# AdaLN-conditioned FFN with LoRA experts on one core: lora_B split a product sooner, the first transposes later, T4's casts in the third group

## The chip, the cores and the metric

The kernel runs on one core of one Trainium2 chip. The metric is the device time of one execution in microseconds; lower is better. All numbers below are of the kernel before the change.

## The reference

```python
h = einsum('bct,bcd->bdt', x, weights[condition])      # (64, 64, 1024), a 64x64 matrix per sample
logits = h @ gate_w.T + expert_bias                     # 4 experts, top 1 by argmax
base   = einsum('bth,oh->bto', h, W_up)                 # 1024 x 1024
z      = einsum('nh,erh->ner', h, lora_A)               # rank 8 for each of 4 experts
delta  = einsum('ner,ehr->neh', z, lora_B) * 1.0, of the chosen expert alone
out    = x + base + delta
```

All of it is in float32. Two samples together make one tile of 128 rows, so there are 32 row tiles ("rows" below) of 128 x 1024.

## The kernel before

The order of the two linear maps is turned round. First x is multiplied with one wide matrix w, which holds the gate (4 columns), lora_A (32) and W_up (1024), 1060 columns in all. The result u is then multiplied, row tile by row tile, with a block-diagonal matrix `bd` of the two samples' 64 x 64 matrices. That gives the logits, the low-rank z and the base output together.

Float32 precision comes from splitting every operand into a high part (float32r, a cast on ACT) and a low part (a subtraction on DVE), and from three matmuls per product: high x high, low x high, high x low. In the profile the tiles named `hB`, `lB`, `hT`, `lT` are the two parts of blocks of w, `ah` and `al` those of x, `uh` and `ul` those of u, `b` those of lora_B.

The rows go in 16 groups g of two (a and b). In a group, x is a 2 x 2 grid of blocks (A11, A12 for row a, A21, A22 for row b; halves of the 1024 input columns) and w a 2 x 2 grid (B11 to B22, halves of 530 output columns). Groups 0 and 1 (`eight`) take eight block products. Groups 2 to 15 (`seven`) take seven, a Strassen-like scheme with sums S1 to S4 of x's blocks and T1 = B12 - B11, T3 = B22 - B12, T2 = B22 - T1, T4 = B21 - T2 of w's blocks. The T blocks are made once, during groups 0 and 1: `begin_b` loads a block from an SP queue, `next_b` negates it in place on ACT (profile: ACT ACTIVATE T<-T) and then adds another block with an accumulating DMA that POOL issues, and `split_b` makes the high and low parts. Each block has four tiles (k = 0 to 3) of 128 x 530. T2 reuses T1's raw tiles, and T4 reuses T2's. T4 shares its split tiles with B12.

One block product is a "step" s of `product`, with four slices k, each of six matmuls (0.74 us at full clock). The order of all other work is written out by hand: `at(s, k, fn, ...)` makes `fn` be issued right after slice k of step s (k = -1: before the step), and `each` does so for several tiles. Every engine executes its own instructions in that program order. So where a call stands decides what it queues behind on ACT, DVE, POOL and PE.

```python
def product(c, g, a, b, first, hooks):
    for k in range(KH):
        ...                       # six matmuls
        for kk, fn, *args in hooks:
            if kk == k:
                fn(*args)
```

What follows a finished u of a row: `apply` (three matmuls with `bd`, into `o`), `gate` (seven small DVE instructions that choose the expert and leave the masked z), `turn` (PE transposes z; ACT copies it to `zt`, DVE makes the low part), `delta` (one matmul with `b3`, lora_B stacked three times, added to the same `o`), `evict` (ACT copies `o` to `y`; after the third column part POOL adds x by an accumulating DMA and SP writes the output). `finish` is apply, delta and evict. `split_b3` makes b3 on ACT (96 x 1024) and its low part on DVE (32 x 1024) from the raw tile `b3f`, which SP loads in three DMAs.

The steps of group 0 that the change touches are 4 (A11 x B12), 5 (A21 x B12), 6 (A12 x B22) and 7 (A22 x B22). In group 2, T4 is read by the seventh product. `load_half` loads half a row tile of x (`xh`, six buffers); `split_a` makes its two parts.

Of the kernel before, what the change touches and what calls it, by code (L numbers as in the profile page):

```python
# [44 lines left out]
def kernel(  # L45
# [131 lines left out]
    def body(c):  # L177
        return c[:, LEFT : LEFT + NB]
# [7 lines left out]
    def u_split(i, n, src):  # L186
        h, lo = u_tiles(i)
        scalar.copy(h[:, n], src)
        vector.tensor_sub(lo[:, n], src, h[:, n].bitcast(F32))

    def half(hf):
        return slice(NB * hf, NB * hf + NB)

    def u_of(i, hf, c):
        u_split(i, half(hf), body(c))
# [5 lines left out]
    def u_sum(i, hf, c, t):  # L201
        u_add(i, c, t)
        u_split(i, half(hf), ts["u", i])
# [168 lines left out]
    def run(g, order, hooks, c):  # L372
        for s, (n, l, r, first) in enumerate(order):
            if first:
                c[n] = chain()
            for kk, fn, *args in hooks[s]:
                if kk < 0:
                    fn(*args)
            product(c[n], g, l, r, first, hooks[s])
# [4 lines left out]
    def eight(g):  # L384
        a, b = 2 * g, 2 * g + 1
        h = [[] for _ in range(8)]

        def at(s, k, fn, *args):
            h[s].append((k, fn, *args))

        def each(s, k, fn, q, ks, *args):
            for i in ks:
                at(s, k, fn, q, i, *args)

        one, two = (0, 1), (2, 3)
        if g == 0:
            at(0, 0, split_a, g, "A21")
            each(0, 1, split_b, "B21", one)
            at(0, 2, split_a, g, "A12")
            each(0, 3, split_b, "B21", two)  # L400
            each(1, -1, load_b, "B12", range(KH))
            at(1, 0, split_a, g, "A22")
            each(1, 1, split_b, "B12", one)
            each(1, 3, split_b, "B12", two)
            each(1, 3, load_b, "B22", range(KH))
            at(2, 1, split_cond, a)
            at(2, 2, load_b3)
            for i in (2, 3):
                at(2, 3, load_half, i, 0)
            at(3, -1, lambda: u_of(a, 0, c["1"]))  # L410
            at(3, 1, split_cond, b)
            each(3, 2, split_b, "B22", one)
            each(3, 2, begin_b, "T1", range(KH), "B11")
            at(3, 3, apply, a, 0)
            at(3, 3, gate, a)
            at(4, -1, lambda: u_of(b, 0, c["2"]))
            each(4, 1, split_b, "B22", two)
            at(4, 3, turn, a)
            each(4, 3, next_b, "T1", one, "B12")
            for i in (2, 3):  # L420
                at(4, 3, load_half, i, 1)
            at(5, 0, split_b3)
            at(5, 1, delta, a, 0)
            at(5, 1, evict, a, 0)
            at(5, 2, apply, b, 0)
            at(5, 2, gate, b)
            each(5, 2, next_b, "T1", two, "B12")
            at(5, 2, split_a, g + 1, "A11")
            each(5, 3, begin_b, "T3", range(KH), "B12")
            at(6, 2, turn, b)  # L430
            at(6, 2, split_a, g + 1, "A21")
            at(7, -1, lambda: u_of(a, 1, c["3"]))
            at(7, 0, delta, b, 0)
            at(7, 0, evict, b, 0)
            at(7, 1, split_a, g + 1, "A12")
            at(7, 2, finish, a, 1)
            each(7, 2, split_b, "T1", one)
            at(7, 3, finish, a, 2)
            order = (
                ("1", "A11", "B11", True),  # L440
                ("2", "A21", "B11", True),
                ("1", "A12", "B21", False),
                ("2", "A22", "B21", False),
                ("3", "A11", "B12", True),
                ("1", "A21", "B12", True),
                ("3", "A12", "B22", False),
                ("1", "A22", "B22", False),
            )
        else:
            p = a - 1  # L450
            at(0, -1, lambda: u_of(p, 1, cs[g - 1]["1"]))
            at(0, 0, split_a, g, "A22")
            at(0, 3, finish, p, 1)
            at(1, 0, finish, p, 2)
            each(0, 3, next_b, "T3", (0, 1, 2, 3), "B22")
            each(1, 1, split_b, "T1", two)
            at(1, 1, load_cond, a + 2)
            at(1, 1, load_cond, b + 2)
            for i in (b + 2, a + 2):
                at(1, 1, load_half, i, 0)  # L460
            each(1, 3, next_b, "T2", one, "B22", "T1")
            each(2, 1, next_b, "T2", two, "B22", "T1")
            for i in (b + 2, a + 2):
                at(2, 1, load_half, i, 1)
            at(3, -1, lambda: u_of(a, 1, c["1"]))
            each(3, 1, split_b, "T3", one)
            each(3, 3, split_b, "T3", two)
            at(4, -1, lambda: u_of(b, 1, c["2"]))
            at(4, 0, sums, g + 1, "S1")
            at(4, 1, split_cond, a)  # L470
            each(4, 1, split_b, "T2", one)
            each(4, 2, next_b, "T4", one, "B21", "T2")
            at(4, 3, split_cond, b)
            at(5, 0, sums, g + 1, "S2")
            each(5, 1, split_b, "T2", two)
            each(5, 2, next_b, "T4", two, "B21", "T2")
            at(5, 2, split_a, g + 1, "A11")
            at(5, 3, sums, g + 1, "S3")
            at(6, 1, split_a, g + 1, "S2")
            at(6, 2, sums, g + 1, "S4")  # L480
            at(7, -1, lambda: u_of(a, 0, c["3"]))
            each(7, 1, split_b, "T4", one)
            at(7, 3, apply, a, 0)
            at(7, 3, gate, a)
            order = (
                ("1", "A11", "B12", True),
                ("2", "A21", "B12", True),
                ("1", "A12", "B22", False),
                ("2", "A22", "B22", False),
                ("3", "A11", "B11", True),  # L490
                ("1", "A21", "B11", True),
                ("3", "A12", "B21", False),
                ("1", "A22", "B21", False),
            )
        run(g, order, h, c)
        cs[g] = dict(c)


    def seven(g):
        a, b = 2 * g, 2 * g + 1  # L500
# [5 lines left out]
        def at(s, k, fn, *args):  # L506
            h[s].append((k, fn, *args))

        def each(s, k, fn, q, ks, *args):
            for i in ks:  # L510
                at(s, k, fn, q, i, *args)
# [15 lines left out]
        if g == 2:  # L527
            at(0, -1, lambda: u_of(pb, 0, cp["1"]))
            at(0, 2, turn, pa)
            at(1, 0, delta, pa, 0)  # L530
            at(1, 0, evict, pa, 0)
            at(1, 1, finish, pa, 1)
            at(1, 2, finish, pa, 2)
            each(1, 3, split_b, "T4", (2, 3))
            at(1, 3, apply, pb, 0)
            at(1, 3, gate, pb)
            at(2, 3, turn, pb)
        else:
            at(0, -1, lambda: u_sum(pb, 0, cp["2"], ts["t1"]))
            at(0, 1, finish, pa, 1)  # L540
            at(0, 3, finish, pa, 2)
            at(1, 2, apply, pb, 0)
            at(1, 2, gate, pb)
            at(2, 2, turn, pb)
# [102 lines left out]
    for g in range(2):  # L647
        eight(g)
    for g in range(2, NG):
        seven(g)  # L650
# [44 lines left out]
```

## Time and profile before

| what | us |
|---|---|
| median of 6 runs | 433.7 |
| lowest and highest run | 432.87 and 435.58 |
| profiled execution, its own time | 433.73 |
| its span, first to last instruction | 431.7 |
| PE busy (96% of the span) | 416.0 |
| DVE busy (65%) | 279.6 |
| ACT busy (44%) | 190.5 |
| POOL busy (19%) | 80.2 |

The times of single instructions come from the profiled execution, in us from the start of its span. The mean granted clock of PE over the span is 0.988. In the listings, PE is the matmul engine, PEld its weight loads, ACT the scalar engine, DVE the vector engine, POOL and SP the two that issue DMAs here. A row of a timeline gives start, length, engine, line, operation, output<-inputs and shape, and in square brackets the idle time of that engine just before it with what ended it. Nearly all instructions carry line 41, which is the helper that keeps program order, so tiles' names tell them apart.

### The profile page before, as it was taken

What the parts mean: (1) busy time and instruction counts of PE and PEld (TensorE: products, weight loads), DVE (VectorE), ACT (ScalarE), POOL (GpSimd) and SP (SyncE); (2) the same over time, 40 slices, a digit from 0 to 9 for tenths busy, and PEclk for the clock granted to TensorE, in tenths of its full rate; (3) what the DMA queues carried; (4) which work ended last, traced back from release to release, by engine and by line L of the source; (5) the groups of instructions that cost most, each with busy time, mean ns of one, the idle gap of its engine ahead of it and who ended that gap; (6) DMA issues with size and microseconds to landing.
All of it is one profiled execution on the core that took longest, in us unless ns stands there. A gap on an engine that the chain in (4) does not pass through costs nothing.

```text
span 431.7 us, 8164 instructions
## 1 busy us (share of the span) xinstructions
PE 416.0 (96%) x3187; PEld 412.5 (96%) x3187; DVE 279.6 (65%) x631; ACT 190.5 (44%) x425; POOL 80.2 (19%) x97
## 2 busy tenths in 40 slices
PE   8969994999999999999999999999999999999996
PEld 7869993999999999999999999999999999999995
DVE  4845247576676766766676666667666666767656
ACT  4854745535353334435233444533444353433531
POOL 2430722202102020200202020110202011020000
PEclk9989997999999999999999999999999999999999
DMA  7997998345364643535564453446445344665243
GB/s 212 348 347 174 212 208 153 69 114 143 104 172 128 172 127 84 131 96 162 129 171 128 100 130 94 149 129 170 129 118 133 87 144 118 173 155 145 50 99 146
DMA packets 26598, 63.18 MB, mean 146 GB/s; under 512 B 3552, under 2 KB 4832, under 8 KB 26560
## 3 DMA queue, kind: packets, MB, share of 16 engines
q0 software_dynamic: 7680, 21.13, 28.0%
q1 hardware_dynamic: 18880, 41.53, 26.7%
q8 instruction: 25, 0.41, 0.4%
q14 instruction: 13, 0.11, 0.1%
HBM read 45.87 MB, written 16.78 MB: 145 GB/s over the span
## 4 chain that ended last, share of the span: by engine, by line
PE 82%; issue 7%; DMA 5%; POOL 3%; DVE 1%; SPq 1%; ACT 0%; POOLq 0%; DVEq 0%
PE c L41 68%; PE o L41 14%; DMA T<-in_w_dram 4%; POOL wsel L41 1%; POOL T L41 1%; DMA cond_sb<-in_cond_dram 1%; SPq L327 0%; SPq L139 0%; DVE S L41 0%; DVE y L41 0%; DVE usum L41 0%; DVE lT L41 0%; DVE ul L41 0%; ACT hT L41 0%; ACT ah L41 0%
## 5 line engine op out<-in xcount | busy, mean ns | idle before, releaser
L41 PE MATMUL c<-hT,ah 128*128 128x264 f32 x480 | 140.5, 293 | 0.0
L41 PE MATMUL c<-lT,ah 128*128 128x264 f32 x480 | 137.9, 287 | 0.0
L41 PE MATMUL c<-hT,al 128*128 128x264 f32 x480 | 137.8, 287 | 0.0
L41 PE MATMUL c<-hB,ah 128*128 128x264 f32 (+1 forms) x432 | 125.6, 291 | 0.8 <-issue 0.5
L41 PE MATMUL c<-hB,al 128*128 128x264 f32 (+1 forms) x432 | 124.8, 289 | 0.3 <-issue 0.3
L41 PE MATMUL c<-lB,ah 128*128 128x264 f32 (+1 forms) x432 | 124.4, 288 | 0.3 <-DVE lB L41 0.3
L41 PEld LDWEIGHTS c<-lT,ah 128*128 128x128 f32 x480 | 91.6, 191 | 0.0
L41 PEld LDWEIGHTS c<-hT,ah 128*128 128x128 f32 x480 | 91.5, 191 | 0.0
L41 PEld LDWEIGHTS c<-hT,al 128*128 128x128 f32 x480 | 91.4, 191 | 0.0
L41 PEld LDWEIGHTS c<-hB,ah 128*128 128x128 f32 x432 | 82.7, 192 | 1.6 <-ACT ah L41 0.8
L41 PEld LDWEIGHTS c<-lB,ah 128*128 128x128 f32 x432 | 82.8, 192 | 1.0 <-DVE lB L41 1.0
L41 POOL DMA_DIRECT2D y<-in_x_dram x30 | 28.9, 962 | 293.4 <-ACT y L41 293.4
L41 PEld LDWEIGHTS c<-hB,al 128*128 128x128 f32 x432 | 82.3, 190 | 0.6 <-issue 0.5
L41 ACT COPY y<-o 128x354 f32<-128x354 f32 (+2 forms) x90 | 39.9, 443 | 62.1 <-PE o L41 60.3
L41 ACT CAST uh<-usum 128x530 fp32r<-128x530 f32 (+4 forms) x44 | 27.1, 616 | 68.8 <-DVE usum L41 68.7
L41 DVE TENSOR_TENSOR al<-xh,ah 128x512 fp32r<-128x512 f32 (+1 forms) x53 | 34.9, 659 | 31.6 <-ACT ah L41 31.6
L41 DVE TENSOR_TENSOR al<-S,ah 128x512 fp32r<-128x512 f32 x56 | 38.5, 687 | 23.5 <-ACT ah L41 23.5
L41 PE MATMUL o<-uh,bd 128*128 128x354 f32 (+2 forms) x188 | 46.6, 329 | 4.9 <-ACT uh L41 4.8
L41 ACT CAST zt<-o 96x128 fp32r<-96x128 f32 x32 | 8.4, 262 | 85.5 <-PE o L41 85.5
L41 DVE TENSOR_TENSOR ul<-usum,uh 128x530 fp32r<-128x530 f32 (+4 forms) x44 | 30.0, 683 | 19.3 <-ACT uh L41 19.3
L41 POOL DMA_INDIRECT wsel<-in_cw_dram,idx x32 | 35.3, 1102 | 9.9 <-issue 5.2
L41 PEld LDWEIGHTS o<-uh,bd 128*128 128x128 f32 x188 | 30.0, 192 | 5.3 <-issue 5.3
(59 smaller groups left out, 466.7 us busy)
## 6 DMA issues: line engine op xcount, KB each, us to landing
xh<-in_xt_dram SPq DMA_DIRECT2D x63, 256.0 KB
y<-in_x_dram POOLq DMA_DIRECT2D x30, 512.0 KB, 5.6
out_dram<-y SPq DMA_DIRECT2D x30, 512.0 KB
wraw<-in_w_dram SPq DMA_DIRECT2D x16, 265.0 KB
T<-in_w_dram POOLq DMA_DIRECT2D x16, 265.0 KB, 7.4
T<-in_w_dram SPq DMA_DIRECT2D x8, 265.0 KB
y<-in_x_dram SPq DMA_DIRECT2D x2, 512.0 KB
wsel<-in_cw_dram,idx POOLq DMA_INDIRECT x32, 4.9
```

Source lines behind the costliest of these rows:

```text
L41: return lambda *a, **k: self.tc.keep_in_program_order(fn(*a, **k))
```

## The change

In group 0 the split of lora_B (`split_b3`) is issued in step 4 after slice 1, ahead of the last two tiles of B22; it was in step 5 after slice 0, behind T1's first two negations. Those last two B22 splits go from slice 1 to slice 2 of step 4. Row a's transpose, T1's first two negations with their POOL DMAs, and two loads of x go from step 4's last slice to step 5's first. Row a's delta and evict go one slice later (step 5, slice 2). Row b's apply and gate go from step 5, slice 2, to step 6, slice 0; T1's second pair and a split of A11 go one slice later. Row b's transpose goes to slice 3 of step 6, its delta and evict to slice 1 of step 7.

In group 1 the split of T4's first two tiles after slice 1 of step 7 is taken out. In group 2 the first two tiles are split in step 1 after slice 3, where the second two were, and the second two in step 2 after slice 3, registered ahead of row pb's transpose.

The work done, the number of DMAs and the order of the DMA issues on SP and POOL are the same. On PE five blocks change place: row a's transpose and delta stand one slice (six matmuls) later, row b's apply two slices, and row b's transpose and delta one slice.

```diff
@@ eight, g == 0
-            each(4, 1, split_b, "B22", two)
-            at(4, 3, turn, a)
-            each(4, 3, next_b, "T1", one, "B12")
+            at(4, 1, split_b3)
+            each(4, 2, split_b, "B22", two)
+            at(5, 0, turn, a)
+            each(5, 0, next_b, "T1", one, "B12")
             for i in (2, 3):
-                at(4, 3, load_half, i, 1)
-            at(5, 0, split_b3)
-            at(5, 1, delta, a, 0)
-            at(5, 1, evict, a, 0)
-            at(5, 2, apply, b, 0)
-            at(5, 2, gate, b)
-            each(5, 2, next_b, "T1", two, "B12")
-            at(5, 2, split_a, g + 1, "A11")
+                at(5, 0, load_half, i, 1)
+            at(5, 2, delta, a, 0)
+            at(5, 2, evict, a, 0)
+            at(6, 0, apply, b, 0)
+            at(6, 0, gate, b)
+            each(5, 3, next_b, "T1", two, "B12")
+            at(5, 3, split_a, g + 1, "A11")
             each(5, 3, begin_b, "T3", range(KH), "B12")
-            at(6, 2, turn, b)
             at(6, 2, split_a, g + 1, "A21")
+            at(6, 3, turn, b)
             at(7, -1, lambda: u_of(a, 1, c["3"]))
-            at(7, 0, delta, b, 0)
-            at(7, 0, evict, b, 0)
+            at(7, 1, delta, b, 0)
+            at(7, 1, evict, b, 0)
@@ eight, g == 1
-            each(7, 1, split_b, "T4", one)
@@ seven, g == 2
-            each(1, 3, split_b, "T4", (2, 3))
+            each(1, 3, split_b, "T4", (0, 1))
+            each(2, 3, split_b, "T4", (2, 3))
```

## The prediction

> **What bounds the kernel now.** The page comes first: TensorE (PE) is busy 416.0 of 431.7 us, so only its gaps and the clock it is granted can give time back. The list of waits, cut to PE, shows where the gaps are (columns: who waited and for whom, us in total, times, longest).
>
> ```profile
> PE o L41 <- ACT uh L41: 4.8, 1, 4.8
> PE o L41 <- DVE b L41: 3.4, 1, 3.4
> PE o L41 <- DVE ul L41: 1.1, 1, 1.1
> ```
>
> After 72 us there is no PE wait up to 415 us. The change touches the second row (call it wait A) and moves what leads to the first and third (wait B). The timelines of PE, ACT and DVE show how A comes about (start, length, idle before and its releaser):
>
> ```profile
> 25.13 0.28 PE L41 MATMUL c<-hT,al 128*128 128x266 f32 x1
> 28.83 0.59 PE L41 MATMUL o<-b,zt 96*128 96x318 f32 x1 [3.42 <-DVE b L41]
> ...
> 25.23 1.36 ACT L41 ACTIVATE T<-T 128x530 f32<-128x530 f32 x2 [0.99 <-DMA T<-in_w_dram]
> 26.50 1.03 ACT L41 CAST b<-b3f 96x1024 fp32r<-96x1024 f32 x1
> 29.46 0.43 ACT L41 COPY y<-o 128x318 f32<-128x318 f32 x1 [1.93 <-PE o L41]
> ...
> 27.56 1.21 DVE L41 TENSOR_TENSOR b<-b3f,b 32x1024 fp32r<-32x1024 f32 x1 [2.17 <-ACT b L41]
> ```
>
> The first row's delta matmul needs b3 (lora_B, high and low part). ACT casts b3 only after two negations of T1, which waited for their load until 25.23; DVE subtracts after that; PE stands from 25.41 to 28.83. The table of busy time by stretch gives the price of it and of what follows (PE busy, granted clock in the column before the last two):
>
> ```profile
> 25.41:28.83 3.42, 0.00 (x1) 0.00 (x1) 1.21 (x1) 2.04 (x3) 1.92 (x2) 1.00 1.05 385
> 28.83:32.32 3.49, 3.49 (x15) 3.49 (x16) 0.55 (x4) 2.01 (x4) 1.60 (x2) 0.51 1.09 318
> 69.94:76.70 6.76, 5.64 (x23) 5.18 (x24) 4.96 (x13) 1.43 (x3) 0.00 (x0) 0.50 0.65 149
> ```
>
> After A the PE ran 3.49 us at 0.51 of its clock, after B 6.76 us at 0.50. Wait B is read from the chain of waits and ACT's timeline:
>
> ```profile
> 54.99 11.20 DMA T<-in_w_dram
> ...
> 66.22 0.63 ACT L41 CAST hT<-T 128x530 fp32r<-128x530 f32 x1 [0.83 <-DMA T<-in_w_dram]
> 69.21 0.59 ACT L41 CAST uh<-c 128x530 fp32r<-128x530 f32 x1
> ...
> 69.94 0.93 PE L41 MATMUL o<-uh,bd 128*128 128x354 f32 x2 [4.83 <-ACT uh L41]
> ```
>
> PE ran dry at 65.1 because ACT, in order, stood at T2's fourth tile (landed 66.20), and after it had a cast, two negations and two A casts to do before `uh`. So B's end is set by the accumulating DMAs, not by PE.
>
> **The change, part by part.** *Wait A.* b3's cast now stands before the last two B22 casts. `uh` of row b ends at 21.5 on ACT. The b3 load must have landed: its three issues (15.16 to 16.68) stand before that of T1 (19.63), and in the trace's packet records the last of its 96 packets of 4096 bytes ends at 22.56. I take 22.65 for the cast. It lasts 1.03, ends 23.7; the two B22 casts follow to 24.8 (they start 0.54 apart). PE now transposes in step 5 after k = 0, at 24.4 instead of 23.67, so ACT's zt copy ends at 25.0, before T1's load lands at 25.23: T1's first negations and POOL's first two T1 DMAs (26.18) do not move. DVE: `ul` to 23.75, b3 low 1.15 to the next start, two B22 subtractions 1.24, zt low 0.29: done at 26.45. PE reaches the delta one slice (six matmuls, 0.74) later than before, at 25.93. So A shrinks from 3.42 to about 0.53. A gap of 0.49 at 13.62 left the clock at 1.00, so I charge no half clock; then the 3.49 us at 0.51 go too, worth 3.49 x 0.49 = 1.71. PE's lead entering step 6: 3.42 + 1.71 - 0.53 = 4.60.
>
> *What moves with it.* The y copy comes behind the delta, at 26.9 instead of 29.46, so T1's second negations start at 27.2 instead of 29.78 and POOL's second T1 pair at 28.2 instead of 30.72. Row b's apply and gate now follow k = 0 of step 6: DVE does A11's low part first (28.9 to 29.5), then the gate (1.35), z at 30.9; the transpose after step 6's last slice falls at 31.0: no wait, but no slack either (0 to 0.2). Delta b at 32.5 has its zt at 31.9. The load issues on SP stand in the same order; those that wait for A's low parts come 3 to 4 us sooner.
>
> *Wait B.* Can the DMAs keep pace with a PE that is 4.60 early? T3's negations stand behind a y copy that PE releases (43.84), and the queue's idle time there is what can be squeezed. Its share by stretch:
>
> ```profile
> 36.00:40.00 4.00, 4.00 (x32) 4.00 (x31) 2.14 (x4) 2.54 (x6) 0.00 (x0) 1.00 0.76 223
> 40.00:42.00 2.00, 2.00 (x19) 2.00 (x18) 1.94 (x4) 1.75 (x4) 0.85 (x1) 1.00 0.14 51
> 42.00:44.00 2.00, 2.00 (x17) 2.00 (x16) 0.57 (x1) 0.16 (x1) 0.00 (x0) 1.00 0.62 102
> 46.00:48.00 2.00, 2.00 (x19) 2.00 (x18) 0.64 (x2) 2.00 (x5) 2.00 (x4) 1.00 0.77 135
> 48.00:66.20 18.20, 17.11 (x140) 16.90 (x138) 8.76 (x17) 9.42 (x19) 8.94 (x10) 1.00 0.99 207
> ```
>
> Idle: 4 x 0.24 + 2 x 0.86 + 2 x 0.38 + 2 x 0.23 = 3.90 us; from 48 to 66.2 it is full (0.99). So T2's fourth tile can land at most about 3.9 us earlier (62.3), ACT's tail of 3.7 follows, PE restarts at 66.0. Of the lead of 4.60, 0.70 goes back into a longer wait B. Bounds: all 4.60 passes if packets run faster with fewer rivals; half of 3.90 if the loads that come sooner push T1's accumulations back. I take 3.90, since the stretch from 48 is as full as the one from 20 to 36. The half clock after B I leave as it is.
>
> The Trainium skill, "DMA: Bandwidth & Descriptors", section "Anatomy of one DMA", gives a POOL-issued DMA about 2.0 us plus bytes / 436e3; by that estimate the fourth tile (265 KB) needs 2.6 us and not 11.20, B would vanish, the lead of 4.60 would pass whole, and the sum below would be 429.7. The row of 11.20 at a full queue decides against it here.
>
> *T4's casts.* The first pair leaves ACT (69.70 to 70.77) and DVE (71.85 to 73.09) between waits; on DVE the gate behind it comes 1.24 sooner, but z was ready at 74.5 and its transpose ran at 76.42: gain nothing. The pair takes the place of the second one behind the y copies of the third group's second product: same work there. The second pair goes to the next product's end, on DVE right ahead of the zt low part:
>
> ```profile
> 86.14 0.46 DVE L41 TENSOR_TENSOR bd<-wsel,bd 64x64 fp32r<-64x64 f32 x2
> 86.63 0.29 DVE L41 TENSOR_TENSOR zt<-o,zt 32x128 fp32r<-32x128 f32 x1
> 87.59 0.31 PE L41 MATMUL o<-b,zt 96*128 96x318 f32 x1
> ```
>
> Two subtractions take 1.24 there, DVE has no gap from 82.27 on, so zt is done at 88.16 and the delta, due at 87.59, waits 0.6. T4 is read only by the seventh product, so nothing else is late. Bounds: 0 if DVE finds slack, 1.24 if all of it shows.
>
> *Sum.* -3.42 - 1.71 + 0.53 + 0.70 + 0.60 = -3.30. The profiled execution took 433.73 (span 431.7), the median of the runs is 433.7, so they agree: 430.4.
>
> The Trainium skill, "TensorE: Matmul & The Clock Gate", part 1, says that an idle window of about 3.4 us halves the clock and that the window runs free of the program. By it A's half clock would be a matter of phase and missing in some runs of before: then the lead is 2.89, all of it passes the DMAs, and the sum is 433.7 - 2.89 + 0.60 = 431.4. This trace's 0.51 after a gap of 3.42 is the only row, and the sum goes by it.
>
> **The rivals.** *The lead is absorbed.* T2's fourth tile lands at 66.2 as before because the queue is the bound from 20 us on. Then wait B grows by the whole lead and T4's 0.6 is left: 434.3. For it: share 1.03 to 1.12 in the stretches from 20 to 36. Against: 3.9 us of idle queue between T1 and T2.
> *b3's cast waits for its own load (the slower side).* The profile shows only that the cast did not wait at 26.50. If b3 lands then, the B22 casts and T1's negations stand behind it: b3 low at 28.7, B22 to 29.95, zt 30.25, delta 30.3. A is 4.37, 0.95 longer than now; with T4's 0.6 and no lead: 435.3. It decides from a landing at about 25.6; the issue order and the packets (22.56) speak against it.
> *The short wait in step 5 costs a half clock of its own* (1.71): lead 2.89, 431.4. The gap of 0.49 without one speaks against it.
>
> **How the numbers follow.** 0.3% (1.3 us) is about what a measurement can tell: faster is under 432.4, slower over 435.0. The forecast with its variants (the half clock in step 5 among them) has 0.74, the absorbed lead 0.15, the late b3 load 0.06, and 0.05 is for what I don't see, mostly slower. Low end: all 4.60 passed and T4's wait nil gives 429.1, and half a window less of half clock after B (3.4 x 0.5 / 2 = 0.85) 428.3. High end: half of the queue's idle time used gives 433.73 - 1.95 + 0.60 = 432.4; to leave out no more than 2 in 10 it reaches on towards the absorbed case, 433.6.
>
> **What would show it.** Right: the PE wait for DVE at the first delta under 1 us and clock 1.00 from 26 to 60 us; T1's second POOL pair near 28; T2's fourth tile at 61.5 to 62.7; wait B of 5 to 6 us; a wait of some 0.6 at the delta of the third group's fourth product. Wrong: b3's cast starting after 23.5; T2's landing at 65 or later; a new wait of PE before 60 us.

## The result, and the profile after

The median of the changed kernel is 431.5 us (429.51 to 432.68 over 32 runs), that of the kernel before 433.38 us over 74 runs. The ratio is 0.9953, 95% interval 0.9942 to 0.9964: 2.0 us faster by the ratio. The profiled execution of the changed kernel took 431.26 us with a span of 429.2, against 433.73 and 431.7: 2.5 us less.

PE's waits after the change, from the list of waits (us in total, times, longest):

```profile
PE o L41 <- ACT uh L41: 3.7, 1, 3.7
PE o L41 <- DVE zt L41: 2.9, 3, 2.1
PE o L41 <- DVE ul L41: 1.5, 1, 1.5
```

The row for b3 (3.4) is gone. In its place stands one for `zt`: 2.05 of it at the first delta, 0.64 at the third group's delta. The wait for `uh` fell from 4.8 to 3.7, the one for `ul` rose from 1.1 to 1.5.

The timelines of ACT, DVE and PE around the first delta:

```profile
24.00 1.05 ACT L41 CAST b<-b3f 96x1024 fp32r<-96x1024 f32 x1 [2.50 <-DMA b3f<-in_lb_dram]
24.95 1.16 ACT L41 CAST hB<-wraw 128x530 fp32r<-128x530 f32 x2
...
25.08 1.22 DVE L41 TENSOR_TENSOR b<-b3f,b 32x1024 fp32r<-32x1024 f32 x1 [1.36 <-ACT b L41]
26.32 1.33 DVE L41 TENSOR_TENSOR lB<-wraw,hB 128x530 fp32r<-128x530 f32 x2
27.69 0.29 DVE L41 TENSOR_TENSOR zt<-o,zt 32x128 fp32r<-32x128 f32 x1
...
28.03 0.41 PE L41 MATMUL o<-b,zt 96*128 96x318 f32 x1 [2.05 <-DVE zt L41]
```

b3's cast is 2.5 us sooner than before, and now it waits for its own load until 24.00. All that was put behind it (the B22 pair on both engines, then the zt low part) waits with it.

The stretches with their granted clock (the number before the DMA share and GB/s): behind the first delta, the second wait, and what follows it.

```profile
28.03:32.32 4.29, 4.29 (x33) 4.29 (x34) 1.62 (x6) 2.53 (x5) 2.75 (x4) 1.00 1.01 330
62.38:66.05 3.67, 0.00 (x1) 0.03 (x1) 1.87 (x4) 3.44 (x7) 1.70 (x2) 1.00 0.91 138
67.24:74.07 6.83, 5.98 (x27) 5.97 (x28) 3.17 (x11) 0.78 (x2) 0.00 (x0) 0.50 0.48 118
36.00:48.00 12.00, 12.00 (x96) 12.00 (x95) 4.35 (x7) 9.40 (x19) 6.17 (x7) 1.00 1.00 206
```

The half clock behind the first wait is gone in this execution, the one behind the second is there as before (6.83 us). The DMA share from 36 to 48 us is 1.00; in the kernel before it is 0.68 over the same stretch:

```profile
36.00:48.00 12.00, 12.00 (x95) 12.00 (x94) 5.29 (x9) 8.45 (x18) 3.71 (x6) 1.00 0.68 162
```

T2's fourth tile, in the chain of waits and on ACT:

```profile
51.11 11.19 DMA T<-in_w_dram
```

```profile
62.32 0.63 ACT L41 CAST hT<-T 128x530 fp32r<-128x530 f32 x1 [0.85 <-DMA T<-in_w_dram]
```

It lands 3.9 us sooner (66.20 to 62.3), and PE starts again at 66.05 instead of 69.94, also 3.9 sooner. Not all of that is the change. POOL issues the four T2 DMAs in these rows, the first of before, the second of after:

```profile
52.16 3.70 POOL L41 DMA_DIRECT2D T<-in_w_dram  x4
49.39 3.71 POOL L41 DMA_DIRECT2D T<-in_w_dram  x4
```

The last issue ends at 55.86 before and at 53.10 after, 2.76 sooner. That is PE's lead: its next apply of row a starts at 35.24 instead of 38.01. From the end of that issue to the cast it took 10.4 us before and 9.2 after, and 8.7 to 9.4 in the nine kernels below that leave the additions of x where they are. So 1.1 of the 3.9 us belong to one slow landing in the profiled execution of before. The second wait is 3.2 us, not 4.8, in two kernels below that keep the old order of group 0 (`e2_t4_alone`, `e8_warm_a`).

From PE's restart to the end some 1.5 us are lost again: 0.4 by the longer wait for `ul`, 0.2 by the clock (half of 5.98 us of busy PE instead of half of 5.64), and 0.9 around the third group's delta:

```profile
83.34 1.33 DVE L41 TENSOR_TENSOR lT<-T,hT 128x530 fp32r<-128x530 f32 x2
84.70 0.29 DVE L41 TENSOR_TENSOR zt<-o,zt 32x128 fp32r<-32x128 f32 x1
...
85.04 0.41 PE L41 MATMUL o<-b,zt 96*128 96x318 f32 x1 [0.64 <-DVE zt L41]
```

3.9 - 0.4 - 0.2 - 0.9 = 2.4, against 2.5 between the spans.

### The profile page after: what moved, and what is told of

Read it like the earlier page. It is cut to its first block, busy times and chain, and to the rows that moved or that the text cites. A ratio compares the mean times of both kernels' runs of the same rounds, so it can differ in the third digit from the quotient of the medians.

```text
span 429.2 us, 8166 instructions
## 1 busy us (share of the span) xinstructions
PE 415.2 (97%) x3187; PEld 411.6 (96%) x3187; DVE 279.9 (65%) x631; ACT 190.2 (44%) x425; POOL 81.0 (19%) x97
## 2 busy tenths in 40 slices
DMA packets 26598, 63.18 MB, mean 147 GB/s; under 512 B 3552, under 2 KB 4832, under 8 KB 26560
## 4 chain that ended last, share of the span: by engine, by line
PE 81%; DMA 8%; issue 4%; DVE 3%; SPq 1%; POOL 1%; ACT 1%; POOLq 0%; DVEq 0%
PE c L41 67%; PE o L41 14%; DMA T<-in_w_dram 5%; DMA wraw<-in_w_dram 3%; SPq L139 1%; POOL T L41 1%; DVE lT L41 1%; DVE S L41 0%; ACT hT L41 0%; DVE y L41 0%; DVE al L41 0%; POOL wsel L41 0%; SPq L102 0%; DVE zm L41 0%; DVE usum L41 0%
## 5 line engine op out<-in xcount | busy, mean ns | idle before, releaser
L41 ACT CAST ah<-S 128x512 fp32r<-128x512 f32 x56 | 34.8, 623 | 0.3
```

Of the source, the lines that this page charges most:

```text
L41: return lambda *a, **k: self.tc.keep_in_program_order(fn(*a, **k))
```

## The experiments

Every kernel was timed in five rounds beside the kernel before, whose medians lay at 433.0 to 433.6; ratios are to those runs. With 5 to 12 runs each, single kernels are uncertain by 0.15 to 0.35%. Differences of about 1 us between two of them lie within overlapping intervals; they are read here together with the waits in the profiles.

**The two parts, each alone.** `e1_steps_alone` takes T4's edits back; `e2_t4_alone` makes them alone on the kernel before.

```diff
# e1_steps_alone, on the changed kernel (e2_t4_alone: the same lines the other way on the kernel before)
# group 1
+            each(7, 1, split_b, "T4", one)
# group 2
-            each(1, 3, split_b, "T4", (0, 1))
-            each(2, 3, split_b, "T4", (2, 3))
+            each(1, 3, split_b, "T4", (2, 3))
```

> The change's group 0 part alone; T4's casts stand as before. Theory: the gain is made in group 0 (PE's first wait for b3 is shorter), and T4's second pair ahead of the zt low part costs 0.6 us at the third group's delta. Then this is 0.6 below the changed kernel: 430.9 against 433.4 before, and the delta there waits for nothing. Rival A: the gain comes from T4's first pair leaving ACT and DVE around the second wait; then nothing is left of it: 433.4. Rival B: T4's 0.6 hides in slack; then 431.5, as the changed kernel.

> T4's casts alone moved as the change does; group 0 as before. Theory: 0.6 us slower than before, 434.0, with a wait of 0.6 for the zt low part at the third group's delta and the first two waits unchanged (3.4 and 4.8). Rival A (T4's move makes the gain): 431.5. Rival B (hidden): 433.4.

Measured: the steps alone 430.25 us, ratio 0.9924 (0.9899 to 0.9949); T4 alone 434.53, ratio 1.0019 (1.0005 to 1.0034). The first part gains 3.3 us, the second costs about 1: 0.8 on the kernel before, 1.2 on the steps. Its wait is there in T4 alone as well. The wait at b3 (3.7) remains; the one at `uh` is 3.2, where 4.8 had been expected. From that kernel's PE timeline:

```profile
88.60 0.41 PE L41 MATMUL o<-b,zt 96*128 96x318 f32 x1 [0.63 <-DVE zt L41]
```

With the steps alone the third group's delta has no wait. Rivals A and B of both runs fall.

**Where T4's cost sits.** `e9_t4_behind` is the changed kernel with one line moved: T4's second pair behind the transpose.

```diff
-            each(2, 3, split_b, "T4", (2, 3))
             at(2, 3, turn, pb)
+            each(2, 3, split_b, "T4", (2, 3))
```

> The changed kernel with T4's second pair registered behind the transpose of the third group's row pb instead of ahead of it: the same two casts and subtractions, one place later on ACT and DVE. Theory: the 0.64 us wait at the delta there, and the 0.2 us that PE needs around it to drain and fill again, come from the two subtractions ahead of the zt low part alone; so the wait goes and 0.9 us with it: 430.6, as the steps alone (430.25). Rival (taking T4's first pair from ACT and DVE before the third group costs something too): 431.0 to 431.5 with the wait gone.

Measured: 430.35 us, 0.9934 (0.9909 to 0.9959), 1.1 less than the changed kernel and level with the steps alone (430.25). DVE now makes `zt` first, and the delta has no wait:

```profile
81.81 0.29 DVE L41 TENSOR_TENSOR zt<-o,zt 32x128 fp32r<-32x128 f32 x1
82.13 1.33 DVE L41 TENSOR_TENSOR lT<-T,hT 128x530 fp32r<-128x530 f32 x2
```

So the cost is the order of three DVE instructions in one place. Taking T4's first pair out of group 1 costs nothing that these runs can tell.

**b3's split alone.** `e7_b3_alone` is the kernel before with only that call moved.

```diff
+            at(4, 1, split_b3)
-            each(4, 1, split_b, "B22", two)
+            each(4, 2, split_b, "B22", two)
-            at(5, 0, split_b3)
```

> The kernel before with b3's split alone in its new place (step 4, slice 1, ahead of the last B22 pair); transposes, deltas, applies and T4 stay. Theory: the zt low part still comes at about 28.0 behind b3's load, so the delta, due one slice (0.74) sooner than in the changed kernel, waits 2.8 us, and PE has 0.7 less lead than with the steps alone: 431.0. Rival (the later transposes and deltas do nothing): 430.25, as the steps alone. Rival (they make the gain): 433 or more.

Measured: 431.31 us, 0.9957 (0.9936 to 0.9977). Its first delta waits 2.28 and starts at 27.84. By the ratio that is 1.9 us of gain for the split; the later transposes, deltas and apply bring the other 1.4 (steps alone 3.3), more than the 0.7 that the theory gave them. The two intervals overlap, so the size of the second share is uncertain.

**What b3's place is worth against its load.** `e3_b3_behind` is the changed kernel with the B22 pair ahead of b3 again, `e4_load_sooner` the changed kernel with b3's loads issued ahead of B22's.

```diff
# e3_b3_behind
-            at(4, 1, split_b3)
-            each(4, 2, split_b, "B22", two)
+            each(4, 1, split_b, "B22", two)
+            at(4, 2, split_b3)
# e4_load_sooner
             each(1, -1, load_b, "B12", range(KH))
+            at(1, 0, load_b3)
...
-            at(2, 2, load_b3)
```

> The changed kernel with the last two B22 splits ahead of b3's again (step 4, slice 1; b3 slice 2). In the changed kernel b3's cast waits for its load until 24.0, and the B22 pair queues behind it on ACT and DVE. Here DVE makes b3's low part at about 25.1 to 26.3 and zt's at 26.6, so the first delta waits some 0.7 instead of 2.05. Theory: the accumulating DMAs set the end of the second wait, and their queue has little idle time left, so of 1.3 us of lead about 0.4 passes: 431.1 against 431.5. Rival (PE's lead passes whole): 430.2. Rival (the order ahead of b3 is what made the gain): 433 or more.

> The changed kernel with b3f's three loads issued ahead of B22's on SP instead of behind them. The load lands before 21.5, so b3's cast does not wait (in the changed kernel 2.5 us of idle ACT before it); B22's loads land about 1 us later. Theory as in the run with b3 behind: the first delta waits under 0.8, and about 0.4 of it passes the second wait: 431.1. Rival (lead passes whole): 430.2. Rival (the first wait is not due to the load): the wait stays at 2 us and the time at 431.5.

Measured: e3 430.51 us, 0.9930 (0.9909 to 0.9951); e4 431.44, 0.9950 (0.9930 to 0.9970). In e3 the first delta waits 0.38 and starts at 27.00, 1.03 sooner than in the changed kernel. T2's fourth tile is cast at 61.47 instead of 62.32, so most of the lead passed the second wait: neither the 0.4 of the theory nor all of it. In e4 the cast has no wait for its load, but the work around it is late: ACT waits 1.03 us for a B12 load, and PE waits 1.0 us for a `uh` until 21.55 (ACT):

```profile
19.73 0.63 ACT L41 CAST hT<-wraw 128x530 fp32r<-128x530 f32 x1 [1.03 <-DMA wraw<-in_w_dram]
...
23.53 1.04 ACT L41 CAST b<-b3f 96x1024 fp32r<-96x1024 f32 x1
```

The wait at the delta falls to 0.95, but the delta stands at 28.94, 0.9 later than in the changed kernel. The sooner load was not to be had for nothing: other loads came later for it.

`e5_both` has the steps alone and e3's order.

> The group 0 part alone (T4's casts as before) with the last two B22 splits ahead of b3's. The one run gave 430.25, the other changed only the order and gained 1.0 us on the changed kernel with a lead of 1.03 us at the first delta. Theory now: the lead of PE passes the second wait nearly whole: 429.3, T2's fourth tile lands 0.8 us sooner than with the steps alone. Rival (the DMA queue is full and holds it): 430.0 to 430.3, the landing unmoved and the second wait 1 us longer.

Measured: 428.71 us, 0.9907 (0.9880 to 0.9933). T2's fourth tile is cast at 61.06 instead of 63.18 with the steps alone, and PE's second wait hardly changes (3.5, 3.3 with the steps alone). PE ran dry 2.3 us sooner, 1.1 by the first delta and the rest because this execution has no half-clock stretch behind it. The rival of a full queue falls here: the landing follows PE.

**The half clock behind the first wait.** `e8_warm_a` is the kernel before with matmuls on zeros in the wait.

```diff
+    def stay_warm(n):
+        o = place()
+        for _ in range(n):
+            tensor.matmul(o[:, :P], warm, warm, start=True, stop=True)
...
+            at(5, 1, stay_warm, 48)
             at(5, 1, delta, a, 0)
```

> The kernel before with 48 bf16 matmuls of 128 x 128 on zeros, into a spare bank, right before the first delta, in the time in which PE waits for b3 (2.7 us of work in 3.4 us of wait at full clock). The wait stays, the half clock behind it should not. Theory: in most runs 3.4 us or more at half clock follow the first wait, so this gains 1.3 to 1.7: 432.0. Rival (the half clock there is rare, or the second wait takes it back): 433.4.

Measured: 431.01 us, 0.9948 (0.9929 to 0.9967). The delta still waits for b3 (0.95 behind the filler) and starts at 29.52, and yet 2.2 us (by the ratio; 1.4 to 3.1 by its interval) are gained. PE and clock in two stretches, the filler and what follows the delta (the clock is the number before the last two):

```profile
25.73:28.57 2.84, 2.83 (x48) 2.66 (x47) 0.32 (x1) 2.23 (x3) 1.66 (x2) 1.00 0.96 308
29.50:33.00 3.50, 3.48 (x27) 3.48 (x28) 1.62 (x7) 2.01 (x4) 1.74 (x2) 1.00 1.07 315
```

So the clock behind the first wait is a cost of its own in the runs of before, not only in the profiled one. The 1.71 of the prediction lies inside the interval.

`e11_warm_b` does the same in front of the second wait of e5.

```diff
+            at(7, 3, stay_warm, 60)             (group 1)
             at(7, 3, apply, a, 0)
```

> The run with both (steps alone, B22 pair ahead of b3; 428.7) and 60 bf16 matmuls of 128 x 128 on zeros before the apply that PE waits for at the end of group 1 (3.5 us of work in 3.5 us of wait). Theory: the two half-clock windows behind the second wait (6.83 us, of which PE is busy some 5.7) are its larger price; they go, worth up to 2.8: 426.0. Rival (the remaining 1.1 us wait for ul keeps the clock down, or the matmuls outlast the wait): 428 to 429.

Measured: 428.09 us, 0.9886 (0.9858 to 0.9915), 0.6 below e5 and inside its interval. The filler covers the wait for `uh`, but the wait of 1.5 for `ul` is still there, and a half-clock stretch of 3.41 us (instead of 6.83) begins at 68.65. Near the rival: one gap filled was not enough.

**What sets the second wait.** `e6_x_later` is e5 with the additions of x to the first two rows behind T2's DMAs.

```diff
-        if j == 2:
-            pool.dma_start(ys[i], x[i], accum_op=ALU.add)
-            nc.sync.dma_start(out[i], ys.pop(i))
+        if j == 2 and i > 1:
+            add_x(i)
+
+    def add_x(i):
+        pool.dma_start(ys[i], x[i], accum_op=ALU.add)
+        nc.sync.dma_start(out[i], ys.pop(i))
...
             each(2, 1, next_b, "T2", two, "B22", "T1")
+            at(2, 2, add_x, p - 1)
+            at(2, 2, add_x, p)
```

> As the run with both, and the accumulating DMAs that add x to the first two rows' y (512 KB each, 8 packets of about 0.33 us on every queue engine, so 2.6 us each), with their output DMAs, are issued behind T2's instead of ahead of T3's and T2's. Theory: the queue sets T2's landing, so its fourth tile lands 2.6 to 5 us sooner against the negations before it, the second wait falls from about 3.8 us to under 1.5, and the time goes to 426 to 427.5. Rival (PE sets it, through the y copy that T3's negations stand behind): landing, wait and time as the run with both, 429.3 to 430.

Measured: 428.22 us, 0.9882 (0.9847 to 0.9917). The mechanism is there and the time is not. T2's last casts run at 58.59 without a wait for their load, and the second wait falls to 1.12. But T4's loads now stand behind the additions, and ACT waits for them ahead of the next `uh`, so the next transpose waits for its z (ACT, then PE):

```profile
65.10 0.64 ACT L41 CAST hT<-T 128x530 fp32r<-128x530 f32 x1 [2.10 <-DMA T<-in_w_dram]
...
70.50 0.31 PE L41 MATMUL o<-ident,z 128*96 128x128 f32 x1 [1.53 <-DVE z L41]
```

`e10_all` takes T4's casts out of that place, as the change does, with e9's order.

```diff
# on e6: T4's edits of the change, with
             at(2, 3, turn, pb)
+            each(2, 3, split_b, "T4", (2, 3))
```

> Both orders of step 4 (B22 pair ahead of b3), x added to the first two rows behind T2, T4's first pair in the third group's second product and its second pair behind the transpose. In the run with x later the second wait had fallen to 1.1 us, but T4's first casts then stood at their own load ahead of the next uh on ACT, and the next transpose waited 1.5 us. Theory: with T4's casts out of that place this wait goes too, and 428.2 becomes 426.5. Rival (the late loads only move the wait on to T4's casts in the third group): 428 or more.

Measured: 424.51 us, 0.9787 (0.9763 to 0.9811), more than expected. The transpose has no wait for z, the second wait is 0.5 for `uh` and 1.5 for `ul`, and 3.41 us at half clock remain. T4's move on e5, without the later additions, was not run; on the steps alone it changed nothing that these runs can tell (e9, 430.35 against 430.25).

`e12_sums_later` moves two sums of the next group behind the gate on DVE.

```diff
-            at(5, 3, sums, g + 1, "S3")
             at(6, 1, split_a, g + 1, "S2")
-            at(6, 2, sums, g + 1, "S4")
             at(7, -1, lambda: u_of(a, 0, c["3"]))
             at(7, 3, apply, a, 0)
             at(7, 3, gate, a)
+            at(7, 3, sums, g + 1, "S3")
+            at(7, 3, sums, g + 1, "S4")
```

> The run with all three orders (424.5), with the sums S3 and S4 of group 2 moved behind the gate of group 1's row a on DVE. What is left of the second wait there is 0.5 us for uh and 1.5 us for ul, and on DVE ul stands behind an A split, S3, S2's split and S4, though its uh is ready 1.4 us before it starts. Theory: without the two sums (0.6 each to the next start) ahead of it ul comes 1.2 us sooner; the wait for it falls to 0.3, and with less idle time the half-clock window behind it (3.4 us) becomes rarer: 422.5 to 423.3. Rival (DVE's next work, the A split of S2, or the later S sums hold something else up): 424.5.

Measured: 422.83 us, 0.9770 (0.9744 to 0.9797), the lowest median here, with an interval that overlaps e10's, and 8.7 us below the changed kernel (7.9 by the ratios). The wait for `ul` is 0.3, the wait for `uh` is out of the list, and the core's granted clock over the span is full:

```profile
core 0: 420.3 us, clock 1.000
```

## Why the prediction was right, step by step

*Sign and mechanism.* The gain is made at the first delta: the split alone and the steps alone show it. 430.4 was forecast, 431.5 measured, in the range; the forecast gain was 1.6 times the measured one. Of the signs for it three came (clock 1.00 from 26 to 60 us, T2's fourth tile at 62.3, the 0.64 at the third group's delta) and three did not (the first delta's wait is 2.05, T1's second POOL pair starts at 29.75, the second wait is 3.7).

*Wait A, 3.42 to 0.53: the step that failed, by its size.* It is 2.05. The mis-sized term is "I take 22.65 for the cast": b3's landing, taken from the end of the last data packet (22.56), was 24.00 for ACT. In the changed kernel's packet records the last 4096-byte packet ends at 23.15. So of the 1.35 about 0.6 is the load itself being later, and the rest is the time from the last packet to the released engine: 0.85, where 0.09 had been allowed. That time is 0.8 to 1.0 in all ten profiles in which the cast waited for this load. The prediction named a cast after 23.5 as a sign against it, and that sign came. The rival of the late load was the right mechanism at 24.0, short of its turning point of 25.6. The late cast also moved what the prediction had left in place: T1's first negations start at 26.18 instead of 25.23, and POOL's first T1 DMAs at 27.13 instead of 26.18.

*The half clock of 1.71.* Right in kind for the kernel before, as the filler run shows, and a little large: six matmuls took 1.33 us in that stretch (29.21 to 30.54) against 0.74 at full clock, so 3.41 us of it cost about 1.5, an estimate from these rows. The further step, that a short wait left in step 5 costs none, was made for 0.53; for the 2.05 that came it held by luck. The steps alone have a wait of 1.89 at the same delta, and its profile reads

```profile
28.32:31.73 3.41, 3.41 (x16) 3.41 (x16) 0.69 (x1) 2.52 (x5) 2.51 (x3) 0.50 1.05 350
```

against 1.00 behind a wait of 2.05 in the changed kernel. The traces' clock records show what the luck was. In every profile with more than one half-clock stretch, their starts lie whole multiples of 3.413 us apart, up to the end of the span (before: 28.91, 69.87 and 431.68, that is 12 and 106 of them). Each execution thus has a grid of windows, and these are the two that hold most of the first wait, of the changed kernel and of the steps alone:

```profile
26.28:29.69 3.41, 1.66 (x13) 1.66 (x14) 1.63 (x4) 2.29 (x5) 1.92 (x2) 1.00 0.99 337
24.91:28.32 3.41, 1.52 (x12) 1.30 (x11) 2.84 (x4) 2.50 (x6) 1.13 (x2) 1.00 1.04 374
```

The wait of 2.05 lay across the border at 26.28 and left PE idle for 1.75 us of its window; the wait of 1.89 lay whole in one. Over all fourteen profiles, from 20 to 418 us, no full-speed window with 1.45 us of idle PE or less was followed by a half-clock one, and every one with 1.79 or more was; between them 1.72 was and 1.75 was not. So a wait of about 2 us costs a half-clock stretch in some executions and none in others, which would make the median gain smaller than that of a profiled pair without one. Ahead of 12 us the rule does not hold: in four profiles a half-clock stretch begins at 7.2 to 8.5 us, behind windows with about 1 us idle, and why is open. The prediction put a page's free-running window beside its sum and did not weigh it enough: The Trainium skill, "TensorE: Matmul & The Clock Gate", part 1, makes the half clock a matter of phase, and the grid agrees. The page speaks of an idle window of about 3.4 us; here 1.8 us idle in a window was enough.

*Wait B: 0.70 given back.* Wrong: none of the lead was given back. PE's real lead was 2.7 us and not 4.60 (it ran dry at 62.38 instead of 65.11), and the wait shrank by 1.16. That 1.16 is the slow landing in the profiled execution of before (10.4 us behind its issue, 8.7 to 9.4 elsewhere), so a shorter second wait is not shown to be an effect of the change. The landing came at the forecast 62.3 by chance, a smaller lead and a faster landing together. Nor was 3.9 us a bound: with the same transfers the tile was cast at 61.85, 61.47 and 61.06 in e9, e3 and e5. The share of 0.68 becoming 1.00 over the same stretch shows that the transfers moved forward with PE; it does not show that the queue's room was used up. What sets the landing is both: its issue follows PE, and the queue sets how long it takes from there, for in e6, which took x's additions out of its way, the cast came 7.3 us behind the issue and did not wait. The absorbed rival falls.

*T4, 0.60.* Right place and cause, 0.64 of wait; the price is 0.9 in the profile and about 1 in the medians. What was left out is what PE loses beside the wait: from transpose to the next apply 4.1 us instead of 3.2, of which 0.64 is the wait that the list shows. Here the zt part starts 1.36 us after the pair of subtractions, not 1.24.

*The sum.* The forecast had the lead at -4.60, B at +0.70 and T4 at +0.60. Measured were 2.7 of lead, nothing given back at B and 0.9 for T4; that makes a gain of 1.8, and the medians lie 1.9 apart. In the profiled pair the slow landing of before adds 1.2, and the longer wait for `ul` and the clock take back 0.6. So the number was helped by luck: A's error of 1.9 was met by 0.70 of B that was wrong the other way. The variant with 431.4 came nearest, but not for its reason, since the half clock behind the first wait was there to be gained. The 429.7 that the prediction sets beside its sum counts the lead alone; a second wait that vanished would have given back its 4.83 as well.

## What to carry to other kernels

When a step is moved ahead on an in-order engine, ask when its own input lands, and put behind it nothing that someone else waits for until then: here the same call one slice later, behind the B22 pair, gained about 1 us more (0.9930 against 0.9953, intervals that overlap a little). A late transfer was worth moving here only together with what waits for it in order: moving the additions of x brought 0.5 us between the medians alone, within the noise, and 4.2 together with T4's casts out of the place ahead of `uh`. And a wait is to be priced with the clock behind it: filling one with idle matmuls, without shortening it, gained 2.2 us.

## What the runs showed of the hardware that was not expected

The half-clock stretches in these profiles last 3.41 or 6.83 us, whatever the wait before them, apart from the one that the end of the program cuts short, and they begin on a grid of 3.413 us. A wait of 2.05 us was followed by none, one of 1.89 and one of 2.28 by 3.41 us, one of 3.65 by 6.83. 48 matmuls of 128 x 128 in bf16 took 2.84 us, and the clock stood at 1.00 through them and behind.

The fourth accumulating T2 DMA of 265 KB was cast 10.4 us (before) and 9.2 us (after) behind the end of its issue; in nine other kernels it was 8.7 to 9.4. The 11.20 and 11.19 of the chain of waits count from the start of the issuing instruction, which came 3.9 us sooner in the second. From the last data packet of b3's load to the start of the cast that waited for it, ten profiles show 0.8 to 1.0 us.
